# First image and constants loaded in order of use; the last batch's norm at two tiles per unit, its add one step behind its silu

## The chip, the cores and the metric

The kernel runs on one core of a Trainium2 chip, in fp32 throughout. The metric is device time in microseconds (us) of one execution. The engines of a core run their own instruction streams in program order and wait for each other by semaphores: PE (TensorE, matmuls), ACT (ScalarE, activations), DVE (VectorE), POOL (GpSimd) and SP (SyncE, which here only issues DMAs).

## The reference, cut to what matters

The input x is 4 batches of 128 channels of 128 x 128 images. Two layers follow each other:

```python
# layer 0 (per batch: 16384 tokens of 128 channels)
h1 = relu(xf @ mlp_w1.T + mlp_b1); xm = h1 @ mlp_w2.T + mlp_b2
x_in, z = split(xm @ in_proj_w.T)
u = silu(causal_conv4(x_in) + conv_b)
dt, Bm, Cm = split(u @ x_proj_w.T)
delta = softplus(dt @ dt_proj_w.T + dt_proj_b)
# scan over the 16384 tokens, 256 channels x 16 states
h = h * exp(delta * A) + delta * B * u;  y = sum_s h * C
out = ((y + u * D) * silu(z)) @ out_proj_w.T
x1 = silu(group_norm(out, 4 groups) * gn_w + gn_b) + x
# layer 1 (per batch)
a = relu(agg_w @ group_norm(cat(x1, x1), 32 groups) + agg_b)
w = softmax(mean(a) @ wg_w.T + wg_b)            # 4 weights per batch
X = rfft2(x1)
result = irfft2(X * X * sum_f w[f] * filt[f]) + residual_weight * x1
```

The weights w of a batch need the whole x1 of that batch, so a batch's spectral work can begin only after its norm and its aggregation (a) are done.

## The kernel before, in words

**Setup** (lines 69 to 132). The helper `const` (L71) loads a weight; it takes SP's and ACT's DMA queues in turn, 25 loads in all, and a 26th (`cwb`, L124) goes to SP. Behind the loads stand a few products of constants: `amat` = -exp(alog) (L115, L116), `diag` (L119), the four conv weights `wck` = win x taps (L126), `weff0` (L129, L130). The taps `cwb` lie in a pool that is closed behind L126, and the pools of the first stage are opened after that.

**First stage, `block0`.** Each batch is cut in 32 chunks of 512 tokens, 128 chunks in all. A chunk takes 16 slots; `todo` holds for each slot and phase what is issued there, and the loop at L486 issues slot by slot, phase by phase. `pre(k)` has a chunk's steps ahead of the scan: `load` (L189), the matmul of the first layer and its Relu (L193, L198), xm, z, the convolution, the loads of replicated rows (`bc_load` L252, `rep_load` L310). Then come exponentials on ACT (L390), scans on DVE (L405), products on POOL and DVE (L352, L407). `finish` gives the norm and aggregation of batches 0 to 2, spread over the slots of the batch behind them. The order on each engine is the order of issue (`manual_schedule`).

**Second stage, `block1`.** Its work is 64 units of 8 channels of one batch, three steps to a unit (images 0-2, 3-5, 6-7). At step t the loop at L844 issues for different blocks, in this order:

- `over_h(t)`: PE matmuls into `pa` (L765, one buffer) and ACT's copy `sa` (L767)
- `evict(t-8)` (DVE, L824), `residual(t-9)` (DVE, L837, and every third time a store), `products(t-2)` (DVE, L790, L791, L797 twice), `conjugates(t)` (DVE, L772)
- `over_w(t-1)`: PE (L779, L780) into `px`, then three ACT operations on it (L782 to L784)
- `back_h(t-7)`, `back_w(t-8)`: PE (L818, L819, L830)
- ACT's `term` (L738) and `copies` (L810, L811), POOL's `mix` (L744) and `sums` (L804): in the first step of a unit one term and the copies, in the second two terms, in the third one term. The first of the two terms of the second step writes a tile `wb` of two buffers, and so waits for the products (L797) of that same step.

`over_h(t)` needs `pa` free again, that is the conjugates of step t-1 done.

The last batch has no batch behind it, so its norm and aggregation run inside the first units of this stage, which belong to batches 0 to 2. `finish` gives the steps, called at L689. Tile i of 32 is normed at step 8+i: `norm_act(i)` (ACT, silu, L558, into a PSUM tile of one buffer) is issued behind the other work of its step, and `norm_dve(i)` (DVE, L562 adds x, L563 takes statistics, then a store of x1 at L564) behind it in the same step. Its loads (L552, L553) are issued three steps ahead. Behind the norm come 14 steps for statistics, and 32 steps with one aggregation tile each (L586, L590), from step 54. `spare` (L692) counts these steps in units and sets how many channel groups are first done for batches 0 to 2 alone (`wait`), so that the last batch's weights are ready when its first unit comes. Groups of `wait` other than the last three load their filter a second time later.

Of the kernel before, what the change touches and what calls it, by code (L numbers as in the profile page):

```python
# [26 lines left out]
F32 = mybir.dt.float32  # L27
AF = mybir.ActivationFunctionType
ALU = mybir.AluOpType
# [4 lines left out]
P = 128  # L34
T = 512
DG = 32
# [5 lines left out]
EPS = 1e-5  # L42


@with_exitstack
def kernel(ctx: ExitStack, tc: tile.TileContext, a: dict, out: bass.AP):
    nc = tc.nc
    x = a["x"]
    B, C, H, W = x.shape
    L = H * W  # L50
    NCH = L // T
    DI = a["mlp_w1T"].shape[1]
    NH = DI // P
    NS = (a["x_wT"].shape[1] - a["dt_wT"].shape[0]) // 2
    NG = NS // SQ
    ND = P // DG
    R = a["dt_wT"].shape[0]
    NX = R + 2 * NS
    KC = a["conv_wT"].shape[0]
    HALO = KC - 1  # L60
    WF = W // 2 + 1
    NF = a["wg_wT"].shape[1]

    cpool = ctx.enter_context(tc.tile_pool(name="const", bufs=1))
    dpool = ctx.enter_context(tc.tile_pool(name="dram", bufs=1, space=DRAM))
    spool = ctx.enter_context(tc.tile_pool(name="stats", bufs=2))
    opool = ctx.enter_context(tc.tile_pool(name="outs", bufs=2, space=DRAM))

    loads = [0]

    def const(name, shape, src):  # L71
        t = cpool.tile(shape, F32, tag=name, name=name)
        eng = (nc.sync, nc.scalar)[loads[0] % 2]
        loads[0] += 1
        eng.dma_start(out=t, in_=src)
        return t

    def col(name):

        n = a[name].shape[0] // P  # L80
        return const(name, [P, n], a[name].rearrange("(j p) -> p j", p=P))

    w1 = const("w1", [P, DI], a["mlp_w1T"])
    b1 = col("mlp_b1")
    w2 = const("w2", [P, NH, C], a["mlp_w2T"].rearrange("(j p) c -> p j c", p=P))
    b2 = col("mlp_b2")
    win = const("win", [P, 2 * DI], a["in_wT"])
    cb = col("conv_b")
    wx = const("wx", [P, NH, NX], a["x_wT"].rearrange("(j p) r -> p j r", p=P))
    wdt = const("wdt", [R, DI], a["dt_wT"])  # L90
    bdt = col("dt_b")
    alog = const("alog", [P, NH * NG * ND], a["alog_q"])
    sel = const("sel", [P, DG], a["c_sel"])
    dvec = col("D")
    wo = const("wo", [P, NH, C], a["out_wT"].rearrange("(j p) c -> p j c", p=P))
    gnw = col("gn_w")
    gnb = col("gn_b")
    ident = const("ident", [P, P], a["c_ident"])
    g0 = const("g0", [P, P], a["c_g0"])
    g1 = const("g1", [P, P], a["c_g1"])  # L100
    gam = col("gn_gamma")
    bet = col("gn_beta")
    wagg = const("wagg", [P, 2, C], a["agg_wT"].rearrange("(j p) o -> p j o", p=P))
    bagg = col("agg_b")
    wwg = const("wwg", [P, NF], a["wg_wT"])
    bwg = const("bwg", [P, NF], a["wg_b"].partition_broadcast(P))
    resw = const("resw", [P, 1], a["residual_weight"].partition_broadcast(P))

    eps = cpool.tile([P, 1], F32, tag="eps", name="eps")
    nc.vector.memset(eps, EPS)  # L110
    ones = cpool.tile([P, P], F32, tag="ones", name="ones")
    nc.vector.memset(ones, 1.0)

    amat = cpool.tile([P, NH * NG * ND], F32, tag="amat", name="amat")
    nc.scalar.activation(amat, alog, AF.Exp)  # L115
    nc.vector.tensor_scalar_mul(amat, amat, -1.0)  # L116
    diag = cpool.tile([P, NH, P], F32, tag="diag", name="diag")
    for j in range(NH):
        nc.vector.tensor_scalar_mul(diag[:, j, :], ident, dvec[:, j : j + 1])  # L119

    wck = cpool.tile([P, KC, DI], F32, tag="wck", name="wck")
    with tc.tile_pool(name="taps", bufs=1) as taps:
        cwb = taps.tile([P, KC, DI], F32, tag="cwb", name="cwb")
        nc.sync.dma_start(out=cwb, in_=a["conv_wT"].partition_broadcast(P))  # L124
        for t in range(KC):
            nc.vector.tensor_mul(wck[:, t, :], win[:, 0:DI], cwb[:, t, :])  # L126

    weff0 = cpool.tile([P, C], F32, tag="weff0", name="weff0")
    nc.vector.tensor_scalar_mul(weff0, wagg[:, 0, :], gam[:, 0:1])  # L129
    nc.vector.scalar_tensor_tensor(weff0, wagg[:, 1, :], gam[:, 1:2], weff0, ALU.mult, ALU.add)  # L130
    bias0 = cpool.tile([P, 1], F32, tag="bias0", name="bias0")
    wts = [cpool.tile([P, NF], F32, tag=f"wts{b}", name=f"wts{b}") for b in range(B)]

    x1 = [dpool.tile([C, H, W], F32, tag=f"x1_{b}", name=f"x1_{b}") for b in range(B)]
    x1flat = [t.rearrange("c h w -> c (h w)") for t in x1]
    xflat = x.rearrange("b c h w -> b c (h w)")

    stats, outs = {}, {}
    shared = SimpleNamespace(**{k: v for k, v in locals().items() if k not in ("ctx", "tc")})
    block0(tc, shared)  # L140
    block1(tc, shared)


def block0(tc, s):
# [4 lines left out]
    with ExitStack() as ctx:  # L149
# [13 lines left out]
        def psum(n):  # L163
            return psp.tile([P, T], F32, tag="pp", name=f"pp_{n}")
# [1 line left out]
        def turn_bank(n):  # L166
            return pst.tile([P, T], F32, tag="pt", name=f"pt_{n}")

        pb0 = psum("bias0")
        for j in range(2):  # L170
            nc.tensor.matmul(pb0[:, 0:1], s.wagg[:, j, :], s.bet[:, j : j + 1], start=j == 0, stop=j == 1)
        nc.vector.tensor_add(s.bias0, pb0[:, 0:1], s.bagg)

        st = {}
        stats, outs = s.stats, s.outs

# [4 lines left out]
        def pre(k):  # L181
# [6 lines left out]

            def load():  # L189
                xt = d["xt"] = p1.tile([P, T], F32, tag="xt", name=f"xt_{k}")  # L190
                nc.sync.dma_start(out=xt, in_=s.xflat[b, :, i * T : (i + 1) * T])

            def h1_mm():  # L193
                for j in range(NH):
# [262 lines left out]
        for k in range(n_chunks):  # L457
            for at, phase, f in pre(k) + post(k):
                todo[at + (k - 1) * NP, phase].append(f)
        io = SimpleNamespace(big=p2, bufs=3, small=tiny, psum=psum)  # L460

        def norm(i):
# [29 lines left out]
def group_norm(s, io, b, mat, which, stat, at, then):  # L492


    nc = s.nc
    g = {}

    def small(n, m=1):
        g[n] = io.small.tile([P, m], F32, tag=n, name=f"{n}_{which}_{b}")
        return g[n]  # L500

    def aggregate():
        nc.vector.bn_aggr(small("mv", 2), stat().rearrange("p n q -> p (n q)"))

    def mean_mm():
        ps = g["ps"] = io.psum(f"gm_{which}_{b}")
        nc.tensor.matmul(ps[:, 0:1], mat, g["mv"][:, 0:1], start=True, stop=True)

    def spread_act():
        mv = g["mv"]  # L510
        nc.scalar.copy(small("mean"), g["ps"][:, 0:1])
        q = small("q")
        nc.scalar.activation(q, mv[:, 0:1], AF.Square, scale=-1.0, bias=g["mean"])
        nc.scalar.activation(q, q, AF.Identity, bias=mv[:, 1:2])

    def var_mm():
        ps = g["ps"] = io.psum(f"gv_{which}_{b}")
        nc.tensor.matmul(ps[:, 0:1], mat, g["q"], start=True, stop=True)

    def root_act():  # L520
        nc.scalar.activation(small("rstd"), g["ps"][:, 0:1], AF.Sqrt, bias=s.eps)

    def invert():
        nc.vector.reciprocal(g["rstd"], g["rstd"])
        then(g["mean"], g["rstd"])

    return [
        (at, "dve", aggregate), (at, "end", mean_mm), (at + 1, "act", spread_act), (at + 3, "pe", var_mm),
        (at + 3, "act", root_act), (at + 3, "dve", invert),
    ]  # L530


def finish(s, io, b, first, norm, agg):

# [2 lines left out]
    g = {}  # L539
# [79 lines left out]
    def weights_act():  # L619
        nc.scalar.activation(s.wts[b], g["lg"], AF.Identity, scale=g["total"])  # L620

    todo = group_norm(s, io, b, s.g0, 0, lambda: stats[b], first, start)
    for i in range(NCH):
        at = norm(i)
        todo += [
            (at[0], "pe", partial(norm_load, i)), (at[1], "act", partial(norm_act, i)),
            (at[2], "dve", partial(norm_dve, i)),
        ]
    c = at[2] + 5
    todo += group_norm(s, io, b, s.g1, 1, lambda: g["stat"], c, middle)  # L630
    todo += [(c + 4, "pe", bias_mm), (c + 4, "act", bias_act)]
    for i in range(NCH):
        at = agg(i)
# [11 lines left out]
def block1(tc, s):  # L645
# [10 lines left out]
    with ExitStack() as ctx:  # L656
# [12 lines left out]
        def const(name, shape):  # L669
            t = p1.tile(shape, F32, tag=name, name=name)  # L670
            nc.sync.dma_start(out=t, in_=s.a[name])
            return t
# [11 lines left out]
        io = SimpleNamespace(  # L684
            big=pool("big", 4), bufs=4, small=small, psum=lambda n: psf.tile([P, T], F32, tag="pf", name=f"pf_{n}")
        )
        t1 = 8 + NCH + 14
        todo = defaultdict(list)
        steps = finish(s, io, B - 1, 0, lambda i: (5 + i, 8 + i, 8 + i), lambda i: (t1 + i - 3, t1 + i, t1 + i, None))  # L689
        for at, phase, f in steps:  # L690
            todo[at, phase].append(f)
        spare = max(at for at, _ in todo) // 3 + 2  # L692
# [149 lines left out]
        with tc.manual_schedule():  # L842
            load(0)
            for t in range(3 * N + LAG + 3):  # L844
# [10 lines left out]
                over_h(t)  # L855
                evict(t - LAG - 1)
                residual(t - LAG - 2)
                products(t - 2)
                conjugates(t)
                over_w(t - 1)  # L860
# [98 lines left out]
```

## Time and profile before

| what | us | share of the span |
|---|---|---|
| median of four runs (7596.57 to 7600.33) | 7599.16 | |
| the profiled execution | 7598.47 | |
| its span, first to last instruction | 7596.2 | |
| PE busy | 6052.3 | 80% |
| DVE busy | 7093.8 | 93% |
| ACT busy | 6352.8 | 84% |
| POOL busy | 7085.9 | 93% |

The profile lists instructions by source line and engine with the tiles they write and read, how long the engine sat idle just before, and what ended that idle time ("[2.48 <-ACT pf_n L558]": idle for 2.48 us until ACT had finished line 558). The first stage takes the span from 0 to about 6787 us, the second the rest. The granted clock of PE is 1.0 or 0.5 at a time, 0.866 in the mean.

### The profile page before, as it was taken

To read this page: it belongs to the slowest core of one execution; us is meant where nothing else is said; L and a number is where in the kernel's file an instruction comes from. 1 tells how busy PE (TensorE), PEld (TensorE's weight loads), DVE (VectorE), ACT (ScalarE), POOL (GpSimd) and SP (SyncE) were. 2 spreads that over 40 slices of the span, in tenths; PEclk is the share of its full clock that TensorE was granted. 3 is DMA by queue.
4 is the path that set the end of the run, shared out by engine and by line. 5 is a ranking of instruction groups with operands and counts; after the bars stand their busy time and mean duration, and the time that the engine had idled before them with its cause. 6 is when DMAs were issued, how large, how long until landed. Compare 5 with 4: busy or idle time off the path is not lost.

```text
span 7596.2 us, 87576 instructions
## 1 busy us (share of the span) xinstructions
PE 6052.3 (80%) x25908; PEld 2676.6 (35%) x25908; DVE 7093.8 (93%) x7064; ACT 6352.8 (84%) x12117; POOL 7085.9 (93%) x3228
## 2 busy tenths in 40 slices
PE   7878878887777788887777778877777787867999
PEld 2323223232222223232222223322222222237999
DVE  6999999999999999999999999999999999977787
ACT  7888888888888888888888888888888888866887
POOL 6999999999999999999999999999999999985788
PEclk8888888888888888888888888888888888889999
DMA  4444444445454544444545444444545544447665
GB/s 145 146 154 156 138 160 151 145 150 173 161 182 169 172 167 143 167 160 166 178 165 183 153 166 165 147 164 163 185 171 173 173 144 165 164 139 225 172 181 158
DMA packets 853743, 1241.87 MB, mean 163 GB/s; under 512 B 76680, under 2 KB 308240, under 8 KB 853264
## 3 DMA queue, kind: packets, MB, share of 16 engines
q1 hardware_dynamic: 851152, 1236.11, 49.5%
q8 instruction: 204, 3.34, 0.2%
q14 instruction: 275, 2.25, 0.1%
q10 hardware_dynamic: 2112, 0.16, 0.0%
HBM read 992.71 MB, written 243.27 MB: 163 GB/s over the span
## 4 chain that ended last, share of the span: by engine, by line
ACT 30%; DVE 26%; PE 17%; POOL 13%; issue 10%; DMA 3%; SPq 1%; DVEq 0%; ACTq 0%; POOLq 0%
ACT da L390 13%; DVE da L405 13%; DVE h L405 7%; POOL hb L352 7%; POOL hb L407 5%; ACT bt L299 5%; PE pp_cv L231 4%; DVE hb L407 3%; ACT L390 3%; PE y L421 2%; POOL du L307 1%; PE pa L765 1%; PE px L780 1%; PE px L779 1%; ACT L270 1%
## 5 line engine op out<-in xcount | busy, mean ns | idle before, releaser
L352 POOL TENSOR_TENSOR hb<-rdu,rB 128x1536 f32<-128x1536 f32 (+2 forms) x1536 | 3608.9, 2366 | 16.2 <-DMA rdu<-dd 16.2
L407 POOL TENSOR_TENSOR hb<-h,rC 128x1024 f32<-128x1024 f32 x1112 | 2629.2, 2367 | 247.7 <-DVE h L405 236.2
L390 ACT ACTIVATE da<-rdelta,amat 128x512 f32<-128x512 f32 x4096 | 2759.8, 700 | 68.1 <-ACT st L408 0.2
L405 DVE TENSOR_TENSOR_SCAN da<-da,st,hb 128x512 f32<-128x512 f32 x1808 | 2317.9, 1282 | 78.5 <-ACT da L390 17.7
L405 DVE TENSOR_TENSOR_SCAN h<-da,st,hb 128x512 f32<-128x512 f32 x1168 | 1456.4, 1258 | 19.2 <-ACT da L390 19.1
L372 PE MATMUL b<-ident,bt 128*128 128x128 f32 x4096 | 773.5, 313 | 878.6 <-DVE h L405 673.9
L421 PE MATMUL y<-hb,sel 128*32 128x512 f32 x8192 | 1379.6, 751 | 1.3 <-POOL hb L407 1.1
L405 DVE TENSOR_TENSOR_SCAN h<-da,st,b 128x512 f32<-128x512 f32 x992 | 1262.2, 1272 | 82.5 <-POOL hb L407 44.0
L299 ACT ACTIVATE bt<-pt_dut,xdt 128x256 f32<-128x256 f32 x2048 | 1190.5, 705 | 62.4 <-PE pt_dut L288 62.1
L407 DVE TENSOR_TENSOR hb<-da,rC 128x1024 f32<-128x1024 f32 x936 | 1146.1, 1224 | 31.9
L231 PE MATMUL pp_cv<-xm,wck 128*128 128x512 f32 x2048 | 1093.0, 682 | 10.3 <-ACT zs L225 10.1
L372 PEld LDWEIGHTS b<-ident,bt 128*128 128x128 f32 x4096 | 537.5, 157 | 1448.0 <-DVE h L405 1031.6
L408 ACT COPY st<-da 128x2 f32<-128x2 f32 x936 | 154.2, 165 | 689.8 <-DVE hb L407 687.9
L231 PEld LDWEIGHTS pp_cv<-xm,wck 128*128 128x128 f32 x2048 | 428.9, 221 | 751.0 <-issue 551.7
L744 POOL TENSOR_TENSOR wb<-wb,term 128x1040 f32<-128x1040 f32 x192 | 461.1, 2402 | 155.4 <-ACT term L738 145.5
L417 PE MATMUL y<-u,diag 128*128 128x512 f32 x512 | 319.3, 709 | 174.4 <-DVE zs L431 174.3
L288 PE MATMUL pt_dut<-ident,du 128*128 128x128 f32 x1024 | 215.0, 345 | 282.2 <-POOL du L307 221.1
L307 POOL TENSOR_TENSOR du<-delta,u 128x512 f32<-128x512 f32 x256 | 319.2, 1269 | 37.0 <-ACT delta L270 37.0
L288 PEld LDWEIGHTS pt_dut<-ident,du 128*128 128x128 f32 x1024 | 139.8, 172 | 601.9 <-POOL du L307 406.0
L408 ACT COPY st<-h 128x2 f32<-128x2 f32 x1112 | 227.1, 204 | 139.4 <-DVE h L405 139.3
L390 ACT ACT_TABLE_LOAD x261 | 334.9, 1283 | 2.9
L196 PE MATMUL pp_h<-xt,w 128*128 128x512 f32 x512 | 304.1, 723 | 22.6 <-DMA xt<-in_x 20.7
(137 smaller groups left out, 8045.6 us busy)
## 6 DMA issues: line engine op xcount, KB each, us to landing
rdelta<-dd SPq DMA_DIRECT2D x1024, 256.0 KB, 3.8
rdu<-dd SPq DMA_DIRECT2D x1024, 256.0 KB, 4.7
rC<-bc SPq DMA_DIRECT2D x512, 256.0 KB, 4.9
rB<-bc SPq DMA_DIRECT2D x384, 256.0 KB, 3.6
dd<-delta SPq DMA_DIRECT2D x256, 256.0 KB, 4.6
dd<-du SPq DMA_DIRECT2D x256, 256.0 KB, 3.9
ft<-in_filt_w SPq DMA_DIRECT2D x96, 520.0 KB, 6.9
xt<-in_x SPq DMA_DIRECT2D x128, 256.0 KB, 4.8
```

Of the source, the lines that this page charges most:

```text
L231: nc.tensor.matmul(ps["cv", j], w, d["xm"][:, t : t + T], start=t == 0, stop=t == KC - 1)
L288: nc.tensor.transpose(ps["dut"][:, 2 * t + j, :], d["du"][:, j, at : at + P], s.ident)
L299: nc.scalar.activation(d["bt"][:, 2 * h + t, :, :, q], src, AF.Copy, scale=d["xdt"][:, 2 * h + t, R + q : R + q + 1])
L307: nc.gpsimd.tensor_tensor(du, d["delta"][:, j, :], d["u"][:, j, :], ALU.mult)
L352: nc.gpsimd.tensor_tensor(hb[:, p : p + n, :], d["du", j][:, m : m + n, :], d["B"][:, p - 1 : p - 1 + n, :], ALU.mult)
L372: nc.tensor.transpose(b[:, t * P : (t + 1) * P], src, s.ident)
L390: nc.scalar.activation(d["da", p][q], d["delta", j][:, m, :], AF.Exp, scale=s.amat[:, c : c + 1])
L405: nc.vector.tensor_tensor_scan(h[:, q, :], das[q], b, init, ALU.mult, ALU.add)
L407: eng.tensor_tensor(hb, h, d["C"][:, p : p + 2, :], ALU.mult)
L408: nc.scalar.copy(last, h[:, :, T - 1])
L421: nc.tensor.matmul(y[m * DG : (m + 1) * DG, :], s.sel, d["hb", j, r][:, p, :], start=False, stop=r == NG - 1)
L744: nc.gpsimd.tensor_tensor(wb, wb, u[n].terms[f], ALU.add)
```

## The change

Setup: the first image's load is the first DMA on ACT's queue (it was on SP's). All constants go to SP's queue. `w1` is loaded at once; 13 more, those that the first chunk needs, are issued behind the first `load` in the first slot, together with the products `wck`, `amat` and `diag` (`first_constants`). The taps are loaded straight into `wck`, and multiplied there. The other 12 loads and two memsets stand at the end of slot 4 of the first chunk's scan (`later_constants`), and the products `weff0` and `bias0` at the end of slot 8 (`later_products`).

Last batch's norm: two tiles in three steps rather than three. Tile i's silu stands in step 9 + 3(i/2) + i%2, that is in the first and second step of a unit; its add and statistics are issued one step later, between `residual` and `products`. The aggregation starts at step 70 (it was 54), `spare` grows from 33 to 38, `wait` from 11 groups to 13, and 26 filter groups are loaded in all (they were 24).

```diff
     def const(name, shape, src):
         t = cpool.tile(shape, F32, tag=name, name=name)
-        eng = (nc.sync, nc.scalar)[loads[0] % 2]
-        loads[0] += 1
-        eng.dma_start(out=t, in_=src)
+        nc.sync.dma_start(out=t, in_=src)
         return t
...
+    def first_constants(s):
+        s.b1 = col("mlp_b1")
+        s.w2 = const("w2", ...)
+        s.b2 = col("mlp_b2")
+        win = s.win = const("win", [P, 2 * DI], a["in_wT"])
+        wck = s.wck = const("wck", [P, KC, DI], a["conv_wT"].partition_broadcast(P))
+        s.cb = col("conv_b")
+        s.wx = const("wx", ...)
+        s.wdt = const("wdt", [R, DI], a["dt_wT"])
+        s.bdt = col("dt_b")
+        s.ident = const("ident", [P, P], a["c_ident"])
+        alog = const("alog", [P, NH * NG * ND], a["alog_q"])
+        dvec = col("D")
+        s.sel = const("sel", [P, DG], a["c_sel"])
+        for t in range(KC):
+            nc.vector.tensor_mul(wck[:, t, :], win[:, 0:DI], wck[:, t, :])
+        amat = s.amat = cpool.tile([P, NH * NG * ND], F32, tag="amat", name="amat")
+        nc.scalar.activation(amat, alog, AF.Exp)
+        nc.vector.tensor_scalar_mul(amat, amat, -1.0)
...
             def load():
                 xt = d["xt"] = p1.tile([P, T], F32, tag="xt", name=f"xt_{k}")
-                nc.sync.dma_start(out=xt, in_=s.xflat[b, :, i * T : (i + 1) * T])
+                (nc.sync if k else nc.scalar).dma_start(out=xt, in_=s.xflat[b, :, i * T : (i + 1) * T])
...
+        todo[min(n for n, _ in todo), "end"].append(partial(s.first_constants, s))
+        todo[4, "end"].append(partial(s.later_constants, s))
+        todo[8, "end"].append(partial(s.later_products, s, psum))
...
-        t1 = 8 + NCH + 14
+
+        def norm(i):
+            t = 9 + 3 * (i // 2) + i % 2
+            return t - 3, t, t + 1
+
+        t1 = norm(NCH - 1)[2] + 14
         todo = defaultdict(list)
-        steps = finish(s, io, B - 1, 0, lambda i: (5 + i, 8 + i, 8 + i), lambda i: (t1 + i - 3, t1 + i, t1 + i, None))
+        steps = finish(s, io, B - 1, 0, norm, lambda i: (t1 + i - 3, t1 + i, t1 + i, None), "mid")
...
                 evict(t - LAG - 1)
                 residual(t - LAG - 2)
+                for f in todo[t, "mid"]:
+                    f()
                 products(t - 2)
                 conjugates(t)
```

More of the change, by code (lines that the diff above doesn't have):

```diff
@@ L67 @@
     opool = ctx.enter_context(tc.tile_pool(name="outs", bufs=2, space=DRAM))
-    loads = [0]
     def const(name, shape, src):
         t = cpool.tile(shape, F32, tag=name, name=name)
-        eng = (nc.sync, nc.scalar)[loads[0] % 2]
-        loads[0] += 1
-        eng.dma_start(out=t, in_=src)
+        nc.sync.dma_start(out=t, in_=src)
         return t
@@ L81, in col @@
         return const(name, [P, n], a[name].rearrange("(j p) -> p j", p=P))
-    w1 = const("w1", [P, DI], a["mlp_w1T"])
[L84 to L128, printed above, removed]
@@ L129 @@
-    nc.vector.tensor_scalar_mul(weff0, wagg[:, 0, :], gam[:, 0:1])
-    nc.vector.scalar_tensor_tensor(weff0, wagg[:, 1, :], gam[:, 1:2], weff0, ALU.mult, ALU.add)
-    bias0 = cpool.tile([P, 1], F32, tag="bias0", name="bias0")
+    def first_constants(s):
+        s.b1 = col("mlp_b1")
+        s.w2 = const("w2", [P, NH, C], a["mlp_w2T"].rearrange("(j p) c -> p j c", p=P))
+        s.b2 = col("mlp_b2")
+        win = s.win = const("win", [P, 2 * DI], a["in_wT"])
+        wck = s.wck = const("wck", [P, KC, DI], a["conv_wT"].partition_broadcast(P))
+        s.cb = col("conv_b")
+        s.wx = const("wx", [P, NH, NX], a["x_wT"].rearrange("(j p) r -> p j r", p=P))
+        s.wdt = const("wdt", [R, DI], a["dt_wT"])
[9 more added lines that the diff above has]
+        nc.vector.tensor_scalar_mul(amat, amat, -1.0)
+        s.diag = cpool.tile([P, NH, P], F32, tag="diag", name="diag")
+        for j in range(NH):
+            nc.vector.tensor_scalar_mul(s.diag[:, j, :], s.ident, dvec[:, j : j + 1])
@@ new lines, in later_constants @@
+    def later_constants(s):
+        s.wo = const("wo", [P, NH, C], a["out_wT"].rearrange("(j p) c -> p j c", p=P))
+        s.gnw = col("gn_w")
+        s.gnb = col("gn_b")
+        s.g0 = const("g0", [P, P], a["c_g0"])
+        s.g1 = const("g1", [P, P], a["c_g1"])
+        s.gam = col("gn_gamma")
+        s.bet = col("gn_beta")
+        s.wagg = const("wagg", [P, 2, C], a["agg_wT"].rearrange("(j p) o -> p j o", p=P))
+        s.bagg = col("agg_b")
+        s.wwg = const("wwg", [P, NF], a["wg_wT"])
+        s.bwg = const("bwg", [P, NF], a["wg_b"].partition_broadcast(P))
+        s.resw = const("resw", [P, 1], a["residual_weight"].partition_broadcast(P))
+        s.eps = cpool.tile([P, 1], F32, tag="eps", name="eps")
+        nc.vector.memset(s.eps, EPS)
+        s.ones = cpool.tile([P, P], F32, tag="ones", name="ones")
+        nc.vector.memset(s.ones, 1.0)
@@ new lines, in later_products @@
+    def later_products(s, psum):
+        weff0 = s.weff0 = cpool.tile([P, C], F32, tag="weff0", name="weff0")
+        nc.vector.tensor_scalar_mul(weff0, s.wagg[:, 0, :], s.gam[:, 0:1])
+        nc.vector.scalar_tensor_tensor(weff0, s.wagg[:, 1, :], s.gam[:, 1:2], weff0, ALU.mult, ALU.add)
+        s.bias0 = cpool.tile([P, 1], F32, tag="bias0", name="bias0")
+        pb0 = psum("bias0")
+        for j in range(2):
+            nc.tensor.matmul(pb0[:, 0:1], s.wagg[:, j, :], s.bet[:, j : j + 1], start=j == 0, stop=j == 1)
+        nc.vector.tensor_add(s.bias0, pb0[:, 0:1], s.bagg)
@@ L167, in turn_bank @@
             return pst.tile([P, T], F32, tag="pt", name=f"pt_{n}")
[L169 to L172, printed above, removed]
         st = {}
@@ L506, in mean_mm @@
         ps = g["ps"] = io.psum(f"gm_{which}_{b}")
-        nc.tensor.matmul(ps[:, 0:1], mat, g["mv"][:, 0:1], start=True, stop=True)
+        nc.tensor.matmul(ps[:, 0:1], getattr(s, mat), g["mv"][:, 0:1], start=True, stop=True)
     def spread_act():
@@ L517, in var_mm @@
         ps = g["ps"] = io.psum(f"gv_{which}_{b}")
-        nc.tensor.matmul(ps[:, 0:1], mat, g["q"], start=True, stop=True)
+        nc.tensor.matmul(ps[:, 0:1], getattr(s, mat), g["q"], start=True, stop=True)
     def root_act():
@@ L530, in group_norm, with finish @@
     ]
-def finish(s, io, b, first, norm, agg):
+def finish(s, io, b, first, norm, agg, add="dve"):
     nc, NCH, C, L, NF = s.nc, s.NCH, s.C, s.L, s.NF
@@ L620, in weights_act @@
         nc.scalar.activation(s.wts[b], g["lg"], AF.Identity, scale=g["total"])
-    todo = group_norm(s, io, b, s.g0, 0, lambda: stats[b], first, start)
+    todo = group_norm(s, io, b, "g0", 0, lambda: stats[b], first, start)
     for i in range(NCH):
@@ L626, in finish @@
             (at[0], "pe", partial(norm_load, i)), (at[1], "act", partial(norm_act, i)),
-            (at[2], "dve", partial(norm_dve, i)),
+            (at[2], add, partial(norm_dve, i)),
         ]
     c = at[2] + 5
-    todo += group_norm(s, io, b, s.g1, 1, lambda: g["stat"], c, middle)
+    todo += group_norm(s, io, b, "g1", 1, lambda: g["stat"], c, middle)
     todo += [(c + 4, "pe", bias_mm), (c + 4, "act", bias_act)]
```

## The prediction

> **What bounds the kernel now.** I read the page first, then the timeline of the first 75 us, then the second stage's: its windows, DVE's waits and one unit's instructions.
>
> The windows (us, then busy us per engine) give each stage's limit.
>
> ```profile
> 500.00:1500.00 1000.00, 797.55 (x2965) 298.40 (x2964) 973.46 (x831) 853.69 (x1605) 977.25 (x439) 0.82 0.45 150
> ...
> 6893.50:6909.90 16.40, 12.29 (x89) 11.72 (x90) 12.59 (x28) 9.44 (x20) 9.57 (x5) 0.90 0.68 209
> 6909.90:6927.90 18.00, 12.79 (x106) 11.84 (x104) 12.67 (x29) 12.48 (x24) 9.82 (x6) 1.00 0.93 270
> ...
> 7232.30:7243.10 10.80, 10.80 (x97) 10.64 (x96) 8.94 (x22) 8.63 (x18) 9.76 (x6) 1.00 1.06 282
> ```
>
> The columns are PE, weight loads, DVE, ACT, POOL, clock, DMA. In the first stage DVE (973 of 1000) and POOL (977) are full: what starts earlier stays earlier, and a microsecond more on DVE costs up to one. In the second stage a plain unit takes 10.8 us and PE is busy all of it. Units with three norm tiles take 16.4 or about 18, and no engine is full. So there a chain of waits decides, not work.
>
> At the start the timeline shows what the first image waits for:
>
> ```profile
> 9.32 0.43 SPq L124 DMA_DIRECT2D cwb<-in_conv_wT  x1
> ...
> 13.44 1.43 DVE L126 TENSOR_TENSOR wck<-win,cwb 128x256 f32<-128x256 f32 x4 [1.60 <-DMA cwb<-in_conv_wT]
> 14.90 0.33 SPq L191 DMA_DIRECT2D xt<-in_x  x1
> 17.70 3.63 PE L196 MATMUL pp_h<-xt,w 128*128 128x512 f32 x4 [6.32 <-DMA xt<-in_x]
> ```
>
> The load of xt goes out 0.03 us after the last product of the taps: its memory was theirs. The first Relu follows at 19.79, the first scan at 59.83.
>
> In the second stage DVE waits for the silu. The waits from 6824 to 6996 (total, times, longest):
>
> ```profile
> DVE of L562 <- ACT pf_n L558: 42.2, 19, 4.1
> ```
>
> One unit of DVE, then of ACT (start, us):
>
> ```profile
> 6953.73 0.69 DVE L562 TENSOR_TENSOR of<-pf_n,xr 128x512 f32<-128x512 f32 x1 [2.48 <-ACT pf_n L558]
> 6954.46 0.69 DVE L563 BATCH_NORM_STATS2 stats<-of 128x6 f32<-128x512 f32 x1
> 6955.07 0.54 DVE L824 COPY sz<-pz 128x384 f32<-128x384 f32 x1
> 6955.52 0.47 DVE L837 SCALAR_TENSOR_TENSOR ot<-xt,resw,po 128x256 f32<-128x256 f32 x1
> 6955.91 0.36 DVE L790 TENSOR_TENSOR sq<-px,xs 128x195 f32<-128x195 f32 x1
> ...
> 6957.73 0.42 DVE L772 TENSOR_TENSOR sa<-pa,c_sign 128x256 f32<-128x256 f32 x1
> 6958.06 0.68 DVE L562 TENSOR_TENSOR of<-pf_n,xr 128x512 f32<-128x512 f32 x1
> ```
>
> ```profile
> 6950.81 1.16 ACT L738 ACTIVATE wb<-ft,wts 128x1040 f32<-128x1040 f32 x1 [2.46 <-DVE pr L797]
> 6951.88 1.15 ACT L738 ACTIVATE term<-ft,wts 128x1040 f32<-128x1040 f32 x1
> 6952.94 0.76 ACT L558 ACTIVATE pf_n<-of,bias,scale 128x512 f32<-128x512 f32 x1
> ...
> 6959.17 0.48 ACT L767 COPY sa<-pa 128x384 f32<-128x384 f32 x1 [2.63 <-PE pa L765]
> ...
> 6960.72 1.15 ACT L738 ACTIVATE term<-ft,wts 128x1040 f32<-128x1040 f32 x1
> ...
> 6962.79 0.78 ACT L558 ACTIVATE pf_n<-of,bias,scale 128x512 f32<-128x512 f32 x1
> ```
>
> The ring of one unit, start to start: add of the second step's tile 6953.73, statistics, evict, residual, products, conjugates, then over_h (PE L765) at 6958.20: 4.47. Copy sa, the three ACT operations, one term, two copies, silu 6962.79, add 6963.60: 5.40. Statistics, evict, residual, products, then wb at 6967.24: 3.64. Two terms and silu to the add, as 6950.81 to 6953.73: 2.92. Sum 16.43, the length of the shorter units. The third step's tile (6958.06) waits for nothing and lies outside the ring.
>
> **The change, part by part.** *First image.* xt now goes out near 0.7 (ACT's first DMA does so now); with 2.67 from issue to landing (14.90 to 17.57) and 2.09 to the first Relu (17.70 to 19.79) PE is ready near 6. What is late next is ACT: `amat`'s Exp stands ahead of that Relu and waits for alog, now twelfth on SP. SP's 14 constants went out from 0.73 to 9.32, 0.66 apart: issue at 8.0, landing 2.7 later, Exp 0.23, Relu at about 10.9, 8.9 earlier. The second Relu waits no more for PE (it came 1.58 behind the first, now 0.7): 9.8 in all, I take **-10**. Bounds: at 0.47 apart, as SP's first four, alog lands at 8.6 and 12 are gained; at 1.0 apart, the widest there, 6. The wck products (taps sixth on SP, 4.1 to land, 1.43) are done near 10 and `diag` and the memset of xm near 12, ahead of xm's need at about 13.
>
> *Later constants.* Twelve DMAs now stand on SP between chunk 1's bc store (76.64) and its loads of rB and rC (78.25), 6 to 8 us by the same spacings; behind them queue both dd stores, chunk 2's xt, rdelta and rdu. The first to need them is POOL at 104.62 (first L352 of chunk 1), whose rdu goes out at 90.66 to 93.1 and lands 4.7 later, near 98: about 7 us of cover. On DVE the products and memsets (0.29, 0.34, 0.16, 0.06, 0.17; they ran in idle time so far) come to 1.0 in a full stage; `bias0`'s add waits for its PE product (0.98) behind the turned du, and DVE's scans behind it wait too: **+1** in all. It is 0 if DVE's waits of 60 to 90 (about 2.6) swallow it, +4 if the cover fails and the queue's excess is paid.
>
> *The norm.* Each add still waits for its silu, on the same ring. But evict and residual now run while DVE waits, ahead of the add: 0.84 (6955.07 to 6955.91) and 0.85 (6948.51 to 6949.36) leave the ring. 16.43 - 1.69 = **14.74 a unit**. Taking the third tile away saves nothing, as it was outside; and 32 tiles now need 16 units, not 10.7. Two waits are added or moved: a silu needs its single PSUM buffer back, that is the add before it, which ends 4 us and more ahead of it in both places of the ring; and SP's store of x1 moves with the add, one step later. Behind that store SP has the next tiles' loads and the unit's xt; a buffer's store now has two steps to land before its next load instead of one, against 4.9 us in the chain of waits (x<-of at 6922.02), so I count nothing.
>
> PE's clock adds to this. The long units hold a half-clock stretch (over_h 1.67 for 0.94): units 3 to 12 average 17.20, 0.77 over the ring. The stretches follow 3.41 us windows in which PE was busy 1.08 to 1.45 (6902.34, 6970.61); one with 1.73 (6885.27) had none behind it. In the new ring PE, from over_h of the third step on, has 3.8 us of work, then idles about 2.2 until the conjugates: a window over that gap holds 1.2. Dips stay possible; I keep 0.77, so 15.5 a unit, between 14.74 (none) and 16.24 (1.5 in each).
>
> The Trainium skill (TensorE: Matmul & The Clock Gate, "What's actually happening") has the clock fall after an idle window of about 3.4 us. By it a 2.2 us gap costs nothing, and the sum would be 12 us less; the rows above show falls after windows 30 to 40% busy, so they decide.
>
> Units 2 to 18 took 6810.2 to 7066.5, 256.3. Now: unit 2 without its tile 10.9 (as unit 14), silu's table load 1.3 on the ring, 16 units, and 4.0 given to later units (statistics 2.3 in unit 15, first aggregation tiles 1.7 in unit 18): 16.2 + 16 x 15.5 = 264.2, **+8** (-4 at 14.74, +20 at 16.24). Two more filter groups, four single-unit groups in a row: stalls like units 38 and 54 (0.4, 0.6): **+1** (0 to 3). The aggregation's own 32 tiles and the tail are unchanged.
>
> Sum: -10 + 1 + 8 + 1 = 0 against the profiled execution's 7598.47, which lies 0.7 under the median: **7598**.
>
> **Rivals.** *The late add frees DVE (faster).* For it: 42.2 us of DVE waits at L562, the very wait that is moved. If ACT could run ahead, a unit would fall to DVE's work, 8.94 + 2 x 1.22 = 11.4: 16.2 + 16 x 11.4 = 198.6, -58, in sum 7533; half of the way, at 13.4, gives 7565. Against: wb waits for the same step's products (2.46), which now stand behind the add.
>
> *Slower paces cost (slower).* A unit's ring may not shorten: if evict and residual wait for PE, or every unit dips, it stays at 17.2. Then 16.2 + 16 x 17.2 = 291.4, +35, in sum 7626. It decides from 16.4 a unit. Against: evict and residual ran without a wait in all rows.
>
> *Part one alone shows.* No dips, 14.74 a unit: -10 + 1 - 4 + 1, 7586. It lies within my case. *The start doesn't do what it says:* the spacing on one queue eats it, -6 only, 7602, also within.
>
> **How the numbers follow.** A measurement of this kernel tells about 0.2%, 15 us, from no change. Forecast (ring 14.7 to 16.3) 0.71, of it nearly all in 7583 to 7613; late add frees DVE 0.21, 7533 to 7583; slower 0.08. The range takes the forecast with its ends (start 6 to 12, ring 14.74 to 16.24) and the faster rival up to half its way, 13.4 a unit: 7565 to 7614, which leaves out about 2 in 10. Faster by over 0.2%: 0.22 (the rival, and a forecast with both best ends); slower: 0.08; within: 0.70.
>
> **What would show it.** Relu L201's counterpart near 11, ahead of it an Exp that waits for alog; the first scan near 50. Units 3 to 18 at 14.7 with some near 16; add waiting for silu about 1.6 in both later steps; half-clock stretches every second or third unit; PE pausing 2 us ahead of the unit's first over_h. If units fall under 14, or DVE stops waiting at the add, the ring is wrong; if they stay above 16.4, the order of evict and residual saves nothing.

## The result, and the profile after

| what | us |
|---|---|
| the kernel after, median of 40 runs (7601.96 to 7619.2) | 7610.61 |
| the kernel before, beside it, median of 60 runs (7588.28 to 7603.34) | 7597.32 |
| ratio after to before, 95% interval | 1.0018 (1.0014 to 1.0022) |
| span of the profiled execution, before and after | 7596.2 and 7608.4 |

The change costs 13 us where 0 was forecast: small, but its interval excludes no change. The two traces show where. The table gives lengths from the two; the second stage's units run from one unit's first conjugates (DVE L772, now L778) to the next one's. Chunks and units are counted from 0, and a chunk has 32 scans.

| stretch | before | after | difference |
|---|---|---|---|
| span's start to the first scan | 59.83 | 51.68 | -8.2 |
| second half of chunk 0, its 17th scan to the first of chunk 1 | 24.25 | 28.57 | +4.3 |
| the rest of the way from the first scan to unit 0 | 6702.8 | 6695.3 | -7.5 |
| units 0 and 1 | 23.3 | 25.3 | +2.0 |
| units 2 to 18 (the norm) | 256.25 | 252.24 | -4.0 |
| units 19 to 44 | 306.7 | 311.9 | +5.2 |
| units 45 to 62 | 194.67 | 215.02 | **+20.3** |

Two rows are chance. From the first scan to unit 0, the thirteen profiled kernels without extra work there took 6723.0 to 6733.0 us, in no order of their setup, so the -7.5 says nothing; for the same reason no single profile tells whether the +4.3 reaches unit 0 whole. Unit 1 was 10.5 to 11.1 in all other profiles, 12.36 only here. Of the +5.2, 1.6 is one unit's chance as well: unit 22 took 12.35 here and 10.8 in all other profiles with two tiles a unit.

The expectations below say "chunk 1" and "chunk 2" for the two ends of the table's second row; by the count of scans these are the 17th and the 33rd scan, chunk 0's second half and chunk 1.

The windows of the kernel after, with PE, weight loads, DVE, ACT, POOL, clock and DMA as before: the first stage, one norm unit, one plain unit.

```profile
500.00:1500.00 1000.00, 799.04 (x2968) 299.30 (x2968) 973.60 (x833) 853.72 (x1602) 977.38 (x440) 0.82 0.44 149
6843.40:6858.10 14.70, 12.16 (x103) 11.78 (x103) 11.37 (x25) 10.23 (x21) 9.70 (x5) 0.98 1.00 306
...
7055.50:7066.30 10.80, 10.80 (x99) 10.80 (x98) 8.93 (x23) 8.84 (x19) 9.67 (x6) 1.00 0.70 181
```

The first stage is as full as it was. The norm unit is 14.7 instead of 16.4, and still no engine fills it: PE, the busiest, works 12.16 of it, DVE 11.37.

The timeline of the start, kernel after (ACTq and SPq are ACT and SP issuing a DMA):

```profile
0.73 0.40 ACTq L189 DMA_DIRECT2D xt<-in_x  x1
...
4.37 3.34 PE L194 MATMUL pp_h<-xt,w 128*128 128x512 f32 x4 [4.37 <-DMA w<-in_mlp_w1T]
...
6.03 0.43 SPq L71 DMA_DIRECT2D alog<-in_alog_q  x1
...
9.26 0.23 ACT L99 ACTIVATE amat<-alog 128x32 f32<-128x32 f32 x1 [6.82 <-DMA alog<-in_alog_q]
9.40 1.25 ACT L199 ACTIVATE h<-pp_h,mlp_b 128x512 f32<-128x512 f32 x2
```

PE no longer waits for the image (17.70 before) but starts at 4.37; what is late next is the Exp, which stands ahead of the Relu on ACT and waits for alog. The Relu comes at 9.40, where it came at 19.79.

DVE's waits in the norm units (6813 to 7013; total, times, longest), and one unit of DVE around the two adds:

```profile
DVE of L563 <- ACT pf_n L559: 37.5, 26, 2.8
```

```profile
6875.23 0.69 DVE L563 TENSOR_TENSOR of<-pf_n,xr 128x512 f32<-128x512 f32 x1 [1.36 <-ACT pf_n L559]
...
6878.83 0.47 DVE L843 SCALAR_TENSOR_TENSOR ot<-xt,resw,po 128x256 f32<-128x256 f32 x1
6880.93 0.69 DVE L563 TENSOR_TENSOR of<-pf_n,xr 128x512 f32<-128x512 f32 x1 [1.64 <-ACT pf_n L559]
```

Evict and residual (L843) now run ahead of the add, but the add still waits in both steps, 1.4 and 1.6 us.

The loss is behind the norm. SP, then ACT, then PE around unit 45, kernel after:

```profile
7359.47 0.38 SPq L846 DMA_DIRECT2D out<-ot  x1
7366.14 3.93 SPq L731 DMA_DIRECT2D ft<-in_filt_w  x4
7370.17 1.88 SPq L737 DMA_DIRECT2D xt<-x  x1
```

```profile
7364.96 1.15 ACT L744 ACTIVATE term<-ft,wts 128x1040 f32<-128x1040 f32 x1
```

```profile
7377.26 1.64 PE L771 MATMUL pa<-c_fh,xt 128*128 128x130 f32 x6 [3.78 <-DMA xt<-x]
```

SP issues nothing from 7359.85 to 7366.14: the filter's four loads go into a buffer whose last reader is ACT's term, which ends at 7366.11. The next unit's xt stands behind them in SP's queue and goes out at 7370.17; PE waits 3.78 us for it and restarts at half clock (1.64 for the 0.83 of a full one). The same happens in units 52/53 and 59/60; the three pairs of units are 6.5 to 7.0 us over two plain ones. SP's waits at the filter loads and PE's for xt, kernel after, from 7320 to 7560 (total, times, longest):

```profile
SPq L731 <- ACT term L744: 18.6, 3, 6.2
```

```profile
PE pa L771 <- DMA xt<-x: 12.3, 3, 4.9
```

In the trace of before no wait of PE for xt is listed in units 45 to 62 (0.5 us in 7320 to 7560), and its filter loads do not wait for a term; SP's longest wait at them there is 1.7 us:

```profile
SPq L725 <- ACT px L784: 5.2, 3, 1.7
```

The lines that set the unit of a load are in `block1`: four units ahead of the filter's first use, or else in the unit of the last use of the filter four loads earlier, whose buffer it takes. Worked out from those lines:

```
                        loads asked in unit, from unit 32 on        last use of the buffer taken
before (11 + 5 groups)  32 36 37 41 42 43 47 48 52 53 54 58 59      3 to 9 units earlier
after  (13 + 3 groups)  32 38 42 43 44 45 49 50 51 52 56 57 58 59   45, 52, 59: the same unit
                                                                    others: 3 to 9 units earlier
```

### The profile page after: what moved, and what is told of

It is laid out like the page before. It is cut to its first block, busy times and chain, and to the rows that moved or that the text cites. A ratio compares the mean times of both kernels' runs of the same rounds, so it can differ in the third digit from the quotient of the medians.

```text
span 7608.4 us, 87598 instructions
## 1 busy us (share of the span) xinstructions
PE 6053.8 (80%) x25908; PEld 2687.2 (35%) x25908; DVE 7097.4 (93%) x7064; ACT 6352.5 (83%) x12117; POOL 7084.9 (93%) x3228
## 4 chain that ended last, share of the span: by engine, by line
ACT 30%; DVE 26%; PE 16%; POOL 13%; issue 10%; DMA 3%; SPq 1%; DVEq 0%; POOLq 0%; ACTq 0%
DVE da L403 13%; ACT da L388 13%; DVE h L403 7%; POOL hb L350 7%; POOL hb L405 6%; ACT bt L297 5%; PE pp_cv L229 4%; DVE hb L405 3%; ACT L388 3%; PE y L419 2%; PE pa L771 1%; POOL du L305 1%; ACT L268 1%; DMA dd<-delta 1%; PE px L786 1%
## 5 line engine op out<-in xcount | busy, mean ns | idle before, releaser
L405 POOL TENSOR_TENSOR hb<-h,rC 128x1024 f32<-128x1024 f32 x1112 | 2628.6, 2367 | 246.9 <-DVE h L403 237.8
L405 DVE TENSOR_TENSOR hb<-da,rC 128x1024 f32<-128x1024 f32 x936 | 1146.1, 1224 | 31.9
```

What stands on the lines that cost most here:

```text
L405: eng.tensor_tensor(hb, h, d["C"][:, p : p + 2, :], ALU.mult)
```

## The experiments

The theory: the setup gains 8 and gives 4 back in two products beside POOL; the norm gains a little; the order of 13 and 3 filter groups costs 20 by SP's wait. The rivals: the stalls come from the late add, the setup, or the bandwidth of the filter loads. "Before" beside the runs was 7596.9 (first four), 7595.3 (next four) and 7595.4 (last four).

**Setup alone**: the new setup with `block1` of before.

```diff
-        def norm(i):
-            t = 9 + 3 * (i // 2) + i % 2
-            return t - 3, t, t + 1
-
-        t1 = norm(NCH - 1)[2] + 14
+        t1 = 8 + NCH + 14
...
```

> Only the new setup (first image first, constants in order of use); the norm's tiles stay three a unit with each add behind its own silu. If the parts add up as the two traces say: the first scan 8 us earlier, chunk 2 only 3 to 4 us earlier because weff0's two products take 2.0 and 2.4 us in place of 0.3 each, second stage as before: 7597 - 4 = 7593 (7588 to 7596), and no unit behind the 44th above 12.5 us. If the setup's gain were lost wholly by the end of the first stage: 7597. If the new constants' order were what stalls units 45, 52 and 59: 7613.

Measured: 7589.9 us, ratio 0.9991 (0.9982 to 1.0). First scan at 51.10, the second half of chunk 0 again long (29.4); units 45 to 62 at 194.2. The setup is a gain of 7 at the edge of the noise (the interval reaches no change), and has no part in the stalls.

**Norm alone**: the new `block1` on the setup of before (the diff is the change's second half).

> Only the norm's two tiles a unit with late adds, on the setup of before. If the filter groups' order (13 and 3 instead of 11 and 5) stalls three units: units 2 to 18 at 252, 4 less than before, units 45 to 63 at 215, 20 more: 7597 + 16 = 7613 (7609 to 7618). If the stalls came from the setup: units 45 to 63 at 195 and 7593 in all.

Measured: 7615.4, ratio 1.0027 (1.0016 to 1.0038); units 2 to 18 at 250.3, units 45 to 62 at 213.5. The two halves, -7.0 and +18.5 by these medians, make 11.6 (unrounded) of the 13.3.

**The filter order alone**: the kernel before, with more waiting groups than it needs.

```diff
-        spare = max(at for at, _ in todo) // 3 + 2
+        spare = 39
```

> The kernel before, with 39 spare units forced in place of 33, so 13 waiting filter groups and 3 others, the after kernel's order; norm and setup unchanged. If this order is the loss: three stalls of near 7 us in units 45, 52 and 59, 7597 + 20 = 7617. If it takes the late add or the slower pace of the norm to make them: within 3 us of 7597, as the prediction's +1 for the filter groups had it.

Measured: 7613.8, ratio 1.0024 (1.0015 to 1.0033). The three stalls are there (14.05 and 13.36, 13.44 and 11.82, 15.50 and 12.48 us for the unit pairs), units 45 to 62 at 210.4. Neither the late add nor the slower pace is needed for them.

**The load asked one unit later**, in the kernel after.

```diff
-                at = max(at, spans[k - KEEP].last)
+                at = max(at, spans[k - KEEP].last + 1)
```

> The kernel after, each filter load asked for one unit behind the last user of its buffer instead of in the same unit, so that the sync engine does not wait for that unit's last term. If the wait at the head of that engine's queue is the loss: the three stalls go, units 45 to 63 at 195, 7610 - 20 = 7590. If the four loads of one filter group in short order are too much for the DMA engines, or three units are too little notice: the stalls move one unit and stay, 7605 or more.

Measured: 7591.9, ratio 0.9995 (0.9986 to 1.0004), 18.7 under the kernel after; units 45 to 62 at 194.7, none above 11.2.

**xt ahead of the filter loads**, in the kernel after: the same waits, another order in the queue.

```diff
+                    load(n + 1)
                     for ft in loads[n]:
                         load_filter(ft)
-                    load(n + 1)
```

> The kernel after, with the next unit's xt asked for ahead of the filter loads of the same unit instead of behind them; the filter loads still wait for the same unit's last term. If PE lost its time because xt stood behind that wait in the sync engine's queue: the three stalls go or shrink to under 1 us each, 7592. If it is the late filter itself or the DMA engines' share: three stalls as before, 7610.

Measured: 7592.1, ratio 0.9997 (0.9988 to 1.0005). SP in this kernel, same place:

```profile
7367.08 0.53 SPq L737 DMA_DIRECT2D xt<-x  x1
7373.27 4.58 SPq L731 DMA_DIRECT2D ft<-in_filt_w  x4
```

And SP's waits at the filter loads in this kernel, from 7310 to 7560:

```profile
SPq L731 <- ACT term L744: 18.3, 4, 5.6
```

SP waits as long as in the kernel after (18.6 there), and PE waits for xt no more. So the wait for the buffer cost nothing in itself; it cost because xt stood behind it. Nor was it the four loads' bandwidth: in the run before this one xt stands behind the same four loads, without the wait, and PE waits for it 0.5 us in all from 7310 to 7550.

**Three tiles a unit with the late add**, on the kernel before: what the second tile's pace is for.

```diff
...
-        t1 = 8 + NCH + 14
+        t1 = 9 + NCH + 14
         todo = defaultdict(list)
-        steps = finish(s, io, B - 1, 0, lambda i: (5 + i, 8 + i, 8 + i), lambda i: (t1 + i - 3, t1 + i, t1 + i, None))
+        steps = finish(s, io, B - 1, 0, lambda i: (5 + i, 8 + i, 9 + i), lambda i: (t1 + i - 3, t1 + i, t1 + i, None), "mid")
...
                 residual(t - LAG - 2)
+                for f in todo[t, "mid"]:
+                    f()
```

> The kernel before with the late add alone: three tiles a unit as before, each add one step behind its silu and ahead of the step's products. Evict and residual leave the ring of waits as in the after kernel, so if the ring decides: units of 14.7 to 15.2 with three tiles where before has 16.4 to 18, over 10.7 units 18 to 25 us less, 7575. If a third tile a unit lengthens the ring in its own right (the reason there could be for two a unit): units stay at 16.4 or more, 7595.

Measured: 7586.4, ratio 0.9988 (0.9979 to 0.9997); a miss by 11. Four of units 3 to 12 took 14.72 with three tiles: a third tile does not lengthen the ring, as the prediction said. But four others took 18.0 to 19.2. The next run shows the same more strongly.

**Three tiles, the add at the next step's end**, on the kernel before: as above with the phase "pe", the first of those issued behind the step's own work, in place of "mid".

> The kernel before with three tiles a unit, each add one step behind its silu but at that step's end, behind products and conjugates. Products then no longer stand behind the add, and wb no longer waits for them: if the add's place ahead of the products is what holds the ring, units fall to the work of DVE, about 13, 45 us less than before, 7552. If a silu's wait for its only PSUM buffer takes over: units stay at 14.7 or more, 7575 or slower.

Measured: 7586.5, ratio 0.9987 (0.9978 to 0.9996); a miss by 34. Units 3 and 4 took 12.8, the other eight norm units 14.0 to 21.8. SP's and PE's waits from 6820 to 6990 in this kernel:

```profile
SPq L553 <- DMA x<-of: 81.9, 28, 4.4
```

```profile
PE pa L765 <- DMA xt<-x: 39.5, 8, 8.5
```

L553 loads a tile into a buffer out of which x1 is just being stored. With four buffers, three tiles a unit and the add one step later, that store was issued in the same step, and SP stands there until it has landed, 2.9 us a time; the unit's xt is again behind it. This was a theory of the miss, so it was tried.

**The same with six buffers for that tile.**

```diff
-            big=pool("big", 4), bufs=4, small=small, psum=lambda n: psf.tile([P, T], F32, tag="pf", name=f"pf_{n}")
+            big=pool("big", 4), bufs=6, small=small, psum=lambda n: psf.tile([P, T], F32, tag="pf", name=f"pf_{n}")
```

> As the run of three late adds at the step's end, with six buffers for the tile that is added and stored, in place of four. If what lengthened its units (18 to 22 in three of ten) was the next tile's load waiting in the sync engine's queue for the store out of its buffer, with the unit's xt behind it: units near 13, about 30 us less, 7555. If three tiles a unit are too much for the DMA engines or for ACT: 7586 as before.

Measured: 7552.7, ratio 0.9947 (0.9933 to 0.9961). Units 3 to 12 are 12.82 or 12.83, all ten, and where SP waited 81.9 us at L553, one wait of 0.3 is left (from 6820 to 6950, where these units end):

```profile
SPq L553 <- DMA xr<-in_x: 0.3, 1, 0.3
```

So two tiles a unit is a pace at which four buffers are enough for a late add. What the pace is worth in itself was not tried alone: units 2 to 62 come to 710.3 here, and to 705.0 in the last run below, which has two tiles a unit but also another filter order.

**Two tiles, the add at the next step's end**, on the kernel after.

```diff
-        steps = finish(s, io, B - 1, 0, norm, lambda i: (t1 + i - 3, t1 + i, t1 + i, None), "mid")
+        steps = finish(s, io, B - 1, 0, norm, lambda i: (t1 + i - 3, t1 + i, t1 + i, None), "pe")
```

> The kernel after with its two tiles a unit, each add moved from ahead of the next step's products to that step's end. If the place ahead of the products holds the ring: units 3 to 18 at 11.4 to 12 in place of 15.1, about 50 less, 7560; the three stalls behind unit 44 stay. If the silu's PSUM buffer holds it: 14.7 a unit, 7610 or slower.

Measured: 7560.1, ratio 0.9954 (0.9942 to 0.9967); units 2 to 18 at 200.6, most norm units 11.49, the three stalls still there. DVE in one unit:

```profile
6879.12 0.55 DVE L778 TENSOR_TENSOR sa<-pa,c_sign 128x384 f32<-128x384 f32 x1
6879.59 0.68 DVE L563 TENSOR_TENSOR of<-pf_n,xr 128x512 f32<-128x512 f32 x1
```

Products and conjugates (L778) come first, the silu is long done when the add comes, and it waits for nothing. The ring of 14.7 was held by the add's place ahead of the products, not by the silu's single PSUM buffer.

**Later constants and their products in the prologue**, in the kernel after, one profiled run.

```diff
-        todo[4, "end"].append(partial(s.later_constants, s))
-        todo[8, "end"].append(partial(s.later_products, s, psum))
+        todo[min(n for n, _ in todo) + 1, "end"].append(partial(s.later_constants, s))
+        todo[-5, "end"].append(partial(s.later_products, s, psum))
```

> The kernel after, with the later constants loaded right behind the first ones and their products (weff0, bias0) made in the prologue, where POOL is idle, in place of chunk 1. If POOL's long operations beside them are what stretched the two products to 1.95 and 2.36 us: 0.3 each here, and chunk 2's first scan 24 to 26 us behind chunk 1's as in the kernel before, 3 to 4 earlier than after. If it was waiting for the constants' landing or the place in DVE's queue: the products are long here too, or the scan stays.

Measured: one run, 7601.6. The two products in the kernel after, at the place the change gave them, with POOL beside them:

```profile
81.74 1.95 DVE L126 TENSOR_SCALAR weff<-wagg,gn_gamma 128x128 f32<-128x128 f32 x1
83.72 2.36 DVE L127 SCALAR_TENSOR_TENSOR weff<-wagg,gn_gamma,weff 128x128 f32<-128x128 f32 x1
```

```profile
80.15 3.45 POOL L350 TENSOR_TENSOR hb<-rdu,rB 128x1536 f32<-128x1536 f32 x1
83.56 2.37 POOL L405 TENSOR_TENSOR hb<-h,rC 128x1024 f32<-128x1024 f32 x1
```

and the first of them in this run, where POOL is idle (the second took 0.35):

```profile
13.57 0.29 DVE L126 TENSOR_SCALAR weff<-wagg,gn_gamma 128x128 f32<-128x128 f32 x1 [3.84 <-DMA wagg<-in_agg_wT]
```

The second half of chunk 0 takes 24.26 (24.27 in the last run below, with the same edit), as before (24.25), against 28.57 after. The loads moved with the products, so the next run looks at the cause. In the rows of the kernel after, POOL's first operation ends at 83.60 and the first product at 83.69; the second ends at 85.93, the second product at 86.08.

**The products repeated** beside POOL: 18 more operations ahead of them, one profiled run.

```diff
+        for _ in range(6):
+            nc.vector.tensor_tensor(weff0, s.wagg[:, 0, :], s.ident, ALU.add)
+        for _ in range(6):
+            nc.vector.tensor_scalar_mul(weff0, s.wagg[:, 0, :], s.gam[:, 0:1])
+        for _ in range(6):
+            nc.vector.scalar_tensor_tensor(weff0, s.wagg[:, 1, :], s.gam[:, 1:2], s.ident, ALU.mult, ALU.add)
```

> The kernel after with 18 more operations of 128x128 on DVE ahead of weff0's first product, at the same place: six plain additions of two SBUF tiles, six products with a column, six of the two-step form (product with a column, then add). They are extra work that nothing needs. If each of the latter two forms waits for POOL's running operation to end: near 2 us each beside POOL, 20 us and more in all, and their ends fall on ends of POOL's operations. If the stretch was one wait, paid once: 0.2 to 0.35 each, under 6 us in all. The plain additions tell whether every form is held.

Measured: one run, 7616.9. The plain additions came first, and four of them met POOL. The timeline of DVE and of POOL around the second:

```profile
83.10 2.35 DVE L127 TENSOR_TENSOR weff<-wagg,ident 128x128 f32<-128x128 f32 x1
```

```profile
82.88 2.42 POOL L411 TENSOR_TENSOR hb<-h,rC 128x1024 f32<-128x1024 f32 x1
```

The four took 2.00, 2.35, 1.23 and 2.32 and ended at 83.07, 85.45, 86.72 and 89.07; POOL's operations ended at 82.92, 85.30, 86.57 and 88.92, each 0.15 earlier. Then POOL, which waits for DVE's scans, ran dry; the fifth and sixth addition took 0.29, and the 12 operations of the other two forms 0.29 and 0.35. So the price was paid again by every operation that met POOL, not once. For the two forms of the kernel itself the five profiles with the products at this place show it, alike (1.93 to 1.95 and 2.36 to 2.37). The 20 us that were expected did not come, because POOL had stopped.

**The three edits together**: the load one unit later, the add at the next step's end, the products in the prologue.

> The kernel after with the three edits that the runs point to: filter loads one unit behind the last user of their buffer (-19), adds at the end of the next step (-50), later constants and products in the prologue (-4). If the gains add: 7611 - 73 = 7538 (7532 to 7545). If the faster norm units bring the filter loads or the DMA queue against each other: 7550 or more.

Measured: 7534.8, ratio 0.992 (0.9907 to 0.9934), 60.5 under before, and the gains add. A norm unit of this kernel:

```profile
6830.70:6842.20 11.50, 10.84 (x95) 10.46 (x93) 11.15 (x26) 10.18 (x21) 9.73 (x5) 1.00 1.08 289
```

DVE works 11.15 of 11.50 and PE 10.84: here the work of an engine nearly fills the unit, and little is left to waits.

## Why the prediction was wrong, step by step

- **First image, -10: right.** The first scan is 8.2 earlier in the profile after, 8.6 to 10.2 in the seven other profiles with the first image on ACT's queue. The named successor, the Exp that waits for alog, is what waits; it came at 9.26 instead of near 10.7 because SP's constants went out 0.48 apart, not 0.66, the pace of the former mixture on two queues. That was the better bound. Not all of it arrives: the second Relu ends 11.4 earlier (10.65, was 22.06), SP's bc store goes out 9.7 earlier (25.69, was 35.43) and the first scan comes 8.2 earlier; no run looks for what is lost on the way.
- **Later constants, +1: wrong in size, +4.3.** The cover of their DMAs held: no wait of POOL for a DMA is listed from 60 to 125. The step "on DVE the products and memsets (0.29, 0.34, 0.16, 0.06, 0.17; they ran in idle time so far) come to 1.0" failed: these rows were taken where POOL was idle too (at 10.37 and 11.50, its last operation having ended before 0.5), and beside POOL the first two cost 1.95 and 2.36.
- **The ring, 14.74 a unit: right.** Units 4, 6, 7, 9, 11, 13, 15, 16 and 18 are 14.72 each, and the waits of the ring are there: the add for the silu (above), and wb for the products, 15.8 us from 6818 to 7006.
- **The clock's share, 0.77 a unit: too high, 0.32.** Units 4 to 18 are 15.04 in the mean, (252.2 - 10.5 - 16.1) / 15. With the 5.2 moved behind unit 18, where 4.0 was expected (3.5 to 5.4 in the five other profiles with this norm), the norm costs about +1 where +8 stood; its bounds held.
- **Filter groups, +1 (0 to 3): wrong, +20.** This alone turns the sign. The step counted the groups ("two more filter groups, four single-unit groups in a row: stalls like units 38 and 54") and priced them by stalls of the trace of before, where no load is asked in the unit that still reads its buffer. It did not ask, for each load, who reads the buffer last and what is queued on SP behind the load. Both stand in the kernel's text. What the runs showed in its place: three loads hold SP for 18.6 us in all, PE waits 12.3 us for the xt behind them and restarts at half clock, and the three pairs of units come out 6.5 to 7.0 us longer each.
- **"So I count nothing" for the stores of x1: right for two tiles a unit.** With three it is the cost, as the runs with four and six buffers show.
- **The rival that the late add frees DVE: rightly put aside**, and for the reason given, wb's wait behind the add. Its price, 11.4 a unit, is what the add at the step's end gave: 11.49.

By its own terms the sum of the profile is -8.2 + 4.3 + 1.2 + 20.3 = 17.6, against 12.2 between the two spans; the difference is the chance rows of the table above, -7.5 and +2.0. That the time still lies within 7565 to 7614 is partly luck: the norm came 7 under its price and the chance rows took another 5.5, which hid more than half of the 20.

The rule on the clock can now be judged too. PE fell to half clock seven times in units 2 to 18 of the kernel after. Four windows of 3.41 us, each two in a row; PE busy stands behind the length, the clock third from the end:

```profile
6867.94:6871.35 3.41, 1.52 (x13) 1.53 (x14) 3.27 (x8) 0.88 (x2) 2.76 (x2) 1.00 0.93 290
6871.35:6874.76 3.41, 3.41 (x32) 3.41 (x31) 2.49 (x6) 3.04 (x7) 1.12 (x1) 1.00 0.19 74
6881.60:6885.01 3.41, 1.43 (x13) 1.23 (x12) 3.24 (x9) 1.43 (x3) 3.23 (x2) 1.00 0.86 209
6885.01:6888.42 3.41, 3.41 (x19) 3.41 (x18) 2.61 (x6) 1.29 (x5) 0.58 (x1) 0.50 1.15 303
```

PE was busy 1.43 of 3.41 us ahead of the half-clock window, and 1.52 ahead of one at full clock. The Trainium skill (TensorE: Matmul & The Clock Gate, "What's actually happening") lets the clock fall after an idle window; by these rows a window 42% busy is enough. In all seven half-clock windows PE was busy throughout, and full clock followed each.

## What to carry to other kernels

When a change alters a planner's order, list for each load the last reader of its buffer and everything queued behind the load on the issuing engine: here a load that waited cost nothing, and a load that waited ahead of an urgent one cost 7 us a time. A late add was off the ring only where it stood behind the work that others waited for. And take a duration only from a row in which the same neighbours were at work.

## What the runs showed of the hardware

- DVE's products and additions on SBUF tiles alone (128x128) took 0.29 to 0.35 us with POOL idle and, in all fourteen cases where POOL was at work (two in each of five profiles, four in the run of repeated products), until 0.08 to 0.15 us behind the end of a POOL operation, 1.23 to 2.37 us. The hot loop's products with an operand in PSUM do not show it (L405, 1.22 to 1.23 beside POOL and without), nor do the statistics of one 128x512 SBUF tile (L563 of the kernel before, 0.69 to 0.70 both ways). The Trainium skill (SBUF — State Buffer, "SBUF: two separate sides") describes it: DVE in such a form and POOL hold a shared pair of ports by turns for a whole instruction; on DVE's side these rows agree.
- Falls of PE's clock in units 2 to 18 of eleven profiles, 68 in all, came behind windows of 3.41 us in which PE was busy 1.50 us or less, but for one (1.85, which I can't explain); no full-clock window without a fall had less than 1.50. In the three profiles with norm units of 11.5 and 12.8 us it did not fall there, and no window had less than 1.99.
- SP issued the first twelve constants, all on its one queue, 0.48 us apart; SP's share of the former mixture on two queues went out 0.66 apart.
